# Gating the second batch's adapters on VectorE, ScalarE and GpSimd during the first FFN

## The chip, the cores and the metric

The kernel runs on one NeuronCore of a Trainium2 chip. The metric is device time in microseconds (us), the median of the runs. The engines are TensorE (PE in the profile, with PEld for its weight loads), VectorE (DVE), ScalarE (ACT), GpSimd (POOL) and the queues that issue transfers, above all SyncE's (SP) and ScalarE's.

## What is computed

For each of two batches of 1024 tokens and 2048 features, x is normalised, quantised and multiplied by a quantised context matrix, and added to itself. The result is normalised again and goes through a linear layer with two low-rank adapters, one of its own and one shared. Each batch is split into four groups of 256 tokens, and each group has its own adapter, a gated sum over 16 stored ones of rank 32:

```python
x = x + matmul(fake_quant(layernorm(x)), fake_quant(ctx))        # ctx: (2, 2048, 2048)
z = layernorm(x)                                                 # eight groups of 256 tokens
A_eff = einsum('bn,nri->bri', gate, lora_A)                      # gate: (8, 16), lora_A: (16, 32, 2048)
B_eff = einsum('bn,nor->bor', gate, lora_B)
delta = einsum('bor,btr->bto', B_eff, einsum('bri,bti->btr', A_eff, z))
delta += the same with lora_A_shared and lora_B_shared
x = x + z @ kernel + bias + delta                                # kernel: (2048, 2048), float32
```

`A_eff` and `B_eff` are what the change is about.

## The kernel before

The batches run one after the other, each with an attention stage and an FFN stage. Part of the second batch's attention is already done in the last pass of the first FFN (`meanwhile`).

**Attention.** `quantise` turns loaded 512 KB pieces of the context into bf16 (ACT L314, DVE L317); `xattn_pair` (L350) multiplies one group of 256 tokens with 512 columns of it: ACT fills PSUM with the constant term (L359), PE runs 32 bf16 matmuls (L361), DVE adds the result to `y` (L370) and takes statistics (L372). Towards the end `prep_z` (L422) normalises a group (DVE L428), PE transposes it (L432), ACT copies it out (L433), and it is stored to `zs` in DRAM (L439).

**Adapters.** `gated` (L376) weighs the 16 stored adapters on PE. The stored rows are loaded so that one matmul with a sparse matrix of gates (`gmat`) sums over all 16 for four groups at once; four such matmuls (L383) give 512 columns of `A_eff` or of `B_eff`. DVE copies the sum out (L395). `lora_a_step` (L398) lets PE transpose it (L403) and DVE put it into `acat` (L406); `lora_b_step` (L411) stores it to the DRAM buffer `bd` with eight small transfers on the SP queue (L416). There are four steps of each kind for each batch, between the pairs of the third and fourth block of columns. Their loads stand in the list `todo` among those of the context. `lora_ax` (L442) then multiplies `z` with `acat` on PE.

**FFN.** `ffn` (L635) runs a product of the Strassen kind twice over: seven outer passes (`OUTER`) of seven inner products (`INNER`), 49 products for each batch, each of eight float32 matmuls of 128x128 by 512 on PE (L611, two records each). Operands are sums or differences of blocks. Those of `w` lie in nine buffers `big` and are combined on DVE, with both inputs in SBUF (L551 for the two-term blocks, L560 for the combinations t1 to t4). Those of `z` lie in ten buffers `lit` and are combined on POOL in the same two lines (s1 to s4). `spread` (L620) adds a finished product from PSUM to one or two places of `y` (DVE L629). `Delta.step` (L466) brings in the adapter term after the products 0, 1, 3 and 4 of the first four passes: bias and `bd` are loaded on the ACT queue (L473, L476), ACT writes the bias to PSUM (L478), PE adds four small products (L483), and DVE adds them to `y` (L493).

**The order.** The tile scheduler puts each engine's instructions in a fixed order when the kernel is built; it may bring an instruction forward of its place in the program. `line` (L499) takes this freedom from the DVE instructions that pass through it: each gets an order edge to the one before. POOL's are not bound by it. In a product's step the order is: combinations of the running pass (`OWN`), combinations for the next pass (`AHEAD`), `spread`, `Delta.step`, two-term blocks for the next pass (`BLOCKS`), then the release of buffers and the next loads on SP (`DROP`, `BEGIN`). The block b21 of the next pass comes after the last product's spread, and PE needs it for the second product of that pass.

Of the kernel before, what the change touches and what calls it, by code (L numbers as in the profile page):

```python
# [20 lines left out]
P = 128  # L21
# [45 lines left out]
def tile_quant_xattn_then_lora_ffn(  # L67
# [56 lines left out]
    st1 = const.tile([P, MT, NN, 6], F32, tag="st1", name="st1")  # L124
    st2 = const.tile([P, MT, NN, 6], F32, tag="st2", name="st2")
    r_s = const.tile([P, MT], F32, tag="r_s", name="r_s")

    zs = [
# [11 lines left out]
    def flat(t):  # L140
        return t.rearrange("p k n -> p (k n)")
# [14 lines left out]
    for b in range(B):  # L156
        for n in range(2):
            todo.extend((b, raw_src(b, n, r)) for r in range(KT // 2))
        for n in range(2, 4):
            for r in range(KT // 2):  # L160
                todo.append((b, raw_src(b, n, r)))
                if r in ((3, 7) if n == 2 else (5, 7)):
                    todo.extend((b, ad_src(la, 2 * (n - 2) + r // 6 if n == 3 else r // 4, h)) for h in range(2))
        for n in range(NN):
            todo.extend((b, ad_src(lb, n, h)) for h in range(2))
    loaded = deque()
    ahead = [2]
# [274 lines left out]
    def lora_ax(b, pr, zqs):  # L442
# [12 lines left out]
                )  # L455
        nc.scalar.copy(axT[:, pr, :], px)

    class Delta:


# [37 lines left out]

    def line(ins):  # L499

        if ins.ins.engine == mybir.EngineType.DVE:
            if line.last is not None:
                tc.add_manual_dep(
                    ins.ins,
                    line.last.name,
                    mybir.DependencyInfo(mybir.DependencyClass.NoSync, mybir.DependencyReason.DATA),
                    reason="line",
                )
            line.last = ins.ins

    line.last = None

    NO = len(OUTER)
    last_use = {}
# [120 lines left out]
    def ffn(b, ops, meanwhile):  # L635

        delta = Delta(b)
        for o in range(NO):
            nxt = Operands(b, o + 1) if o + 1 < NO else None
            chains = {}  # L640
            for s in range(len(INNER)):
                product(b, o, s, ops, chains)
                if s in OWN:
                    OWN[s](ops)
                if nxt and s in AHEAD:
                    AHEAD[s](nxt)
                spread(b, o, s, chains)
                if s in (0, 1, 3, 4):
                    delta.step()
                added = line.last  # L650
                if nxt:
                    for name in BLOCKS.get(s, ()):
                        nxt.block(name)
                for name in DROP.get(s, ()):
                    ops.drop(name)
                if nxt:
                    for name in BEGIN.get(s, ()):
                        nxt.load(name)
                with tc.issue_after(added):
                    meanwhile(o, s)  # L660
            ops = nxt
# [31 lines left out]
    for b in range(B):  # L693
# [30 lines left out]
        for g in range(2, GPB):  # L724
            for m in range(g * MG, (g + 1) * MG):
                with tc.issue_after(opened.ins):
                    prep_x(b, m, c1T, wk)
            for n in range(2):
                xattn_pair(b, n, g, c1T, c2[n])
                if g + 1 == GPB:  # L730
                    close_c2(n)
                    open_c2(n + 2)
                    bp.give(colt.pop(n))
                    if n == 0:
                        for r in range(NR):
                            quantise(c2[2], r)
                            if r % 4 == 3:
                                lora_a_step(b, r // 4)
                        column_term(b, 2, c2[2])
        if b == 0:  # L740
            for pr in range(GPB // 2):
# [12 lines left out]
        lora_b_step(b, 0)  # L754
        close_c2(2)
        bp.give(colt.pop(2))
        first = Operands(b, 0)
# [2 lines left out]
        for g in range(GPB):  # L760
# [149 lines left out]
```

## Time and profile before

| | |
|---|---|
| median of 3 runs | 1127.66 us (1126.64 to 1129.02) |
| profiled execution, its own time | 1128.61 us |
| its span | 1126.8 us |
| busy in the span: PE / DVE / ACT / POOL | 1072.4 / 741.5 / 261.1 / 266.6 us |
| first FFN, 300 to 350 us: PE / DVE / ACT / POOL busy | 50.00 / 38.39 / 3.05 / 19.83 us |
| second attention, 650 to 700 us: the same | 49.13 / 26.74 / 19.07 / 0.00 us |
| second attention, 700 to 750 us: the same | 49.39 / 31.26 / 12.99 / 2.22 us |
| granted TensorE clock | 1.00 in all these stretches |

The first attention lasts to about 232 us, the first FFN to about 582 us with the second batch's attention begun from about 542, the second attention to about 782 us, and the second FFN to the end. A row of the profile gives line, engine, operation and tile with shapes, the number of instructions, their busy time and the mean of one, and the idle time before them with what ended it. In a timeline a row is start, length, engine, line and what is written from what; neighbours of the same kind are merged (x3), and a bracket gives the idle time before. A line can be that of a helper: L551 and L560 stand both for DVE and for POOL.

### The profile page before, as it was taken

The numbers are of one execution on the slowest core, as the hardware profiler recorded it, in microseconds if no ns is written. First come the engines' busy times: TensorE is split into PE (matmuls) and PEld (weight loads), VectorE is DVE, ScalarE is ACT, GpSimd is POOL, SyncE is SP. The second block draws the span as 40 slices with busy tenths as digits, with TensorE's granted clock in tenths as the row PEclk, the third lists the DMA queues.
The fourth block names the chain that finished last, engine by engine and source line by source line (L and its number), as shares of the span: only waits on it lengthen the run. The fifth ranks groups of instructions, "written<-read, shape, count | busy, mean of one in ns | idle before, by whom it ended". The sixth has DMA issues, their size and how long they took to land.

```text
span 1126.8 us, 10619 instructions
## 1 busy us (share of the span) xinstructions
PE 1072.4 (95%) x3926; PEld 489.3 (43%) x3926; DVE 741.5 (66%) x969; ACT 261.1 (23%) x342; POOL 266.6 (24%) x106
## 2 busy tenths in 40 slices
PE   1689899999999999999999999999999999999998
PEld 0244334554444444444444433455444444444443
DVE  4685547576696768568777654766668586865861
ACT  5875513320001010001375761232000000000000
POOL 0000000234253422525000000022535343243600
PEclk9999999999999999999999999999999999999999
DMA  8991935885789757489857094588668875749611
GB/s 307 391 244 35 282 124 217 298 322 205 246 285 377 266 181 264 141 301 355 285 184 228 1 277 154 182 301 314 244 215 293 295 255 181 256 145 322 213 38 56
DMA packets 120772, 261.35 MB, mean 232 GB/s; under 512 B 11920, under 2 KB 16144, under 8 KB 119568
## 3 DMA queue, kind: packets, MB, share of 16 engines
q1 hardware_dynamic: 99264, 218.65, 56.6%
q10 hardware_dynamic: 21456, 42.02, 10.5%
q8 instruction: 31, 0.51, 0.2%
q14 instruction: 21, 0.17, 0.0%
HBM read 224.99 MB, written 37.75 MB: 233 GB/s over the span
## 4 chain that ended last, share of the span: by engine, by line
PE 80%; DMA 7%; DVE 6%; ACT 4%; issue 1%; SPq 1%; ACTq 0%; DVEq 0%
PE fu L611 33%; PE fv L611 17%; PE pa L361 13%; PE fw L611 9%; DMA lit<-in_ctx_dram 4%; PE pl L483 3%; PE ptz L432 2%; DVE big L560 1%; PE pg_a L383 1%; DVE st L283 1%; PE pg_b L383 1%; ACT big L298 1%; ACT big L295 1%; DMA bd<-q2b 1%; DMA big<-in_w_dram 1%
## 5 line engine op out<-in xcount | busy, mean ns | idle before, releaser
L611 PE MATMUL fu<-big,lit 128*128 128x512 f32 x896 | 396.3, 594 | 2.4 <-DVE y L629 2.4
L560 POOL TENSOR_TENSOR lit<-lit,lit 128x1024 f32<-128x1024 f32 x56 | 165.2, 2957 | 539.4 <-PE pa L361 209.1
L611 PEld LDWEIGHTS fu<-big,lit 128*128 128x128 f32 x896 | 167.8, 190 | 208.2 <-issue 206.7
L361 PE MATMUL pa<-big,big 128*128 128x512 bf16 x1024 | 238.0, 382 | 11.9 <-ACT pa L359 10.6
L611 PE MATMUL fv<-big,lit 128*128 128x512 f32 x448 | 198.1, 594 | 0.0
L551 POOL TENSOR_TENSOR lit<-lit,lit 128x1024 f32<-128x1024 f32 x40 | 100.9, 2524 | 283.4 <-DMA lit<-zs 255.5
L560 DVE TENSOR_TENSOR big<-big,big 128x2048 f32<-128x2048 f32 x56 | 159.4, 2850 | 5.9 <-PE ptz L432 5.3
L361 PEld LDWEIGHTS <-big 128*128 128x128 bf16 x1024 | 97.0, 98 | 146.5 <-issue 44.3
L629 DVE TENSOR_TENSOR y<-y,fu 128x1024 f32<-128x1024 f32 (+1 forms) x98 | 113.7, 1194 | 67.2 <-PE fu L611 66.8
L611 PEld LDWEIGHTS fv<-big,lit 128*128 128x128 f32 x448 | 84.3, 190 | 105.0 <-issue 105.0
L629 DVE TENSOR_TENSOR y<-y,fv 128x1024 f32<-128x1024 f32 x48 | 56.8, 1218 | 91.1 <-PE fv L611 91.1
L478 ACT COPY pl<-bias 128x1024 f32<-128x1024 f32 x32 | 32.6, 1017 | 344.9 <-DVE y L493 327.1
L314 ACT ACTIVATE q2b<-lit,sc,inv 128x1024 int16<-128x1024 f32 x64 | 76.6, 1230 | 146.4 <-DMA lit<-in_ctx_dram 124.7
L551 DVE TENSOR_TENSOR big<-big,big 128x2048 f32<-128x2048 f32 x40 | 101.7, 2544 | 13.2 <-DMA big<-in_w_dram 13.2
L611 PE MATMUL fw<-big,lit 128*128 128x512 f32 x224 | 100.6, 596 | 0.1
L370 DVE SCALAR_TENSOR_TENSOR y<-pa,k_s,y 128x1024 f32<-128x1024 f32 x32 | 41.0, 1282 | 69.7 <-PE pa L361 69.7
L359 ACT ACTIVATE pa<-bp,r_s 128x512 f32<-128x512 f32 x64 | 42.8, 684 | 105.6 <-PE pa L361 60.5
L629 DVE TENSOR_TENSOR y<-y,fw 128x1024 f32<-128x1024 f32 x24 | 28.4, 1217 | 52.5 <-PE fw L611 52.5
L611 PEld LDWEIGHTS fw<-big,lit 128*128 128x128 f32 x224 | 41.3, 190 | 48.7 <-issue 48.2
L303 PE MATMUL pt<-ident_h,big 128*128 128x128 bf16 x256 | 20.3, 231 | 29.6 <-ACT big L298 29.4
L283 DVE BATCH_NORM_STATS2 st<-y 128x6 f32<-128x512 f32 x64 | 42.1, 680 | 2.9 <-DMA y<-in_x_dram 2.9
L317 DVE TENSOR_SCALAR big<-q2b 128x1024 bf16<-128x1024 int16 x64 | 27.6, 440 | 23.7 <-ACT q2b L314 20.5
(79 smaller groups left out, 609.9 us busy)
## 6 DMA issues: line engine op xcount, KB each, us to landing
big<-in_w_dram SPq DMA_DIRECT2D x96, 1024.0 KB
lit<-zs SPq DMA_DIRECT2D x88, 512.0 KB
lit<-in_ctx_dram SPq DMA_DIRECT2D x64, 512.0 KB
out_dram<-y ACTq DMA_DIRECT2D x30, 512.0 KB
zs<-lit ACTq DMA_DIRECT2D x24, 512.0 KB
y<-in_x_dram SPq DMA_DIRECT2D x8, 1024.0 KB
lit<-in_lora_a_dram SPq DMA_DIRECT2D x32, 256.0 KB
lit<-in_lora_bt_dram SPq DMA_DIRECT2D x32, 256.0 KB
```

What stands on the lines that cost most here:

```text
L283: nc.vector.bn_stats(st1[:, m, n, :], ym[:, ds(n * NB, NB)])
L314: nc.scalar.activation(qi, t, AF.Relu, bias=z2, scale=inv2)
L317: nc.vector.tensor_scalar(c2[r // 4][:, ds(2 * (r % 4), 2), :], qi, QMAX, CENTRE, ALU.min, ALU.subtract)
L359: nc.scalar.activation(pa[:, j, :], colt[n], AF.Identity, bias=r_s[:, m : m + 1])
L361: nc.tensor.matmul(pa[:, j, :], c1T[g][:, k, ds(j * P, P)], c2[k // 8][:, k % 8, :], start=False, stop=(k == KT - 1), skip_group_check=True,)
L370: summed = nc.vector.scalar_tensor_tensor(yp, pa, s12, yp, ALU.mult, ALU.add)
L478: nc.scalar.copy(pl, self.bb.unsqueeze(1).to_broadcast([P, 2, NB]))
L483: nc.tensor.matmul(pl[:, i, ds(h * (NB // 2), NB // 2)], axT[rows, pr, ds(j * P, P)], self.bp[rows, ds(h * (NB // 2), NB // 2)], start=Fal ...
L551: line(eng.tensor_tensor(got[0], got[0], got[1], ALU.add if terms[1][2] > 0 else ALU.subtract))
L560: line(eng.tensor_tensor(out_t, at[p], at[q], op))
L611: nc.tensor.matmul(ps[:, m, :], at[:, k, ds(m * P, P)], bt[:, k, :], start=(opens and k == 0), stop=(ends and k == KQ - 1), skip_group_che ...
L629: line(nc.vector.tensor_tensor(yp, yp, chains[chain][:, js, :], ALU.add if sign > 0 else ALU.subtract))
```

## The change

For the second batch the gated sums are formed without matmuls, during the first batch's FFN. A new class `Gates` takes one step after each product. In products 0 to 15 it loads one stored B adapter each (256 KB, SP queue), and one product later adds it to the accumulators of the four groups, which lie in `acat`: for two groups DVE does a fused multiply and add, for the other two ACT multiplies into a spare buffer and POOL adds. Then the sums go to `bd` with one copy and one transfer a group on ACT. From product 18 the A adapters follow in the same way, and in products 35 to 38 each group's sum is transposed on PE (`turn`), with a copy on ACT before and after. The buffers are a ring of four of 512 columns: the three `q2b` and the statistics buffer, now one tile.

The DVE and POOL instructions of `Gates` pass through `line`, and `line` now keeps an order for POOL too, in both FFNs. `gate_b`, which was overwritten with masked gates, is loaded once more on SP during the first attention. For the second batch `lora_a_step`, `lora_b_step` and their loads are left out; the first batch keeps them.

```diff
+    st = const.tile([P, NB], F32, tag="st", name="st")
+    st1, st2 = (st[:, ds(i * MT * NN * 6, MT * NN * 6)].rearrange("p (m n s) -> p m n s", n=NN, s=6) for i in range(2))
...
-                if r in ((3, 7) if n == 2 else (5, 7)):
+                if b == 0 and r in ((3, 7) if n == 2 else (5, 7)):
...
-        for n in range(NN):
+        for n in range(NN if b == 0 else 0):
...
+    class Gates:
+        OWN = (2, 2, 2, 2, 2, 2, 2)
+        def __init__(self, b):
+            self.b = b
+            self.slot = 0
+            self.held = deque()
+            self.bufs = [q2b.take() for _ in range(len(q2b.spare))]
+            self.ring = Bufs([st] + [flat(t).bitcast(F32) for t in self.bufs])
+        def acc(self, g):
+            return acat[:, :, own_col[g], :]
+        def load(self, src, n):
+            t = self.ring.take()
+            nc.sync.dma_start(out=t, in_=src[ds(n * R, R), :].rearrange("r (c i) -> (r c) i", i=NB))
+            self.held.append(t)
+        def add(self, o, n):
+            t = self.held.popleft()
+            tv = t.rearrange("p (k r) -> p k r", r=R)
+            for g in range(GPB):
+                gw = gate_b[:, self.b * GPB + g, n : n + 1]
+                if g >= self.OWN[o]:
+                    if n == 0:
+                        nc.scalar.mul(self.acc(g), tv, gw)
+                        continue
+                    tmp = self.ring.take()
+                    nc.scalar.mul(tmp, t, gw)
+                    line(
+                        nc.gpsimd.tensor_tensor(
+                            self.acc(g), self.acc(g), tmp.rearrange("p (k r) -> p k r", r=R), ALU.add
+                        )
+                    )
+                    self.ring.give(tmp)
+                elif n == 0:
+                    line(nc.vector.tensor_scalar(self.acc(g), tv, gw, None, ALU.mult))
+                else:
+                    line(nc.vector.scalar_tensor_tensor(self.acc(g), tv, gw, self.acc(g), ALU.mult, ALU.add))
+            self.ring.give(t)
+        def store(self, gs):
...
+        def turn(self, g):
+            t = self.ring.take()
+            nc.scalar.copy(t.rearrange("p (k r) -> p k r", r=R), self.acc(g))
+            pt = ps_m.tile([P, KQ, P], F32, tag="pm", name=f"pgt_{self.b}_{g}")
+            for k in range(KQ):
+                nc.tensor.transpose(pt[:, k, :], t[:, ds(k * P, P)], ident)
...
+        def step(self, o):
+            s = self.slot
+            self.slot += 1
+            if s < NL:
+                self.load(lora_bt, s)
+            if 1 <= s < NL + 1:
+                self.add(o, s - 1)
+            if s == NL + 1:
+                self.store(range(GPB))
+            s -= NL + 2
+            if 0 <= s < NL:
+                self.load(lora_a, s)
+            if 1 <= s < NL + 1:
+                self.add(o, s - 1)
+            if NL + 1 <= s < NL + 1 + GPB:
+                self.turn(s - NL - 1)
...
     def line(ins):
-        if ins.ins.engine == mybir.EngineType.DVE:
...
+        eng = ins.ins.engine
+        if eng in line.last:
...
     def ffn(b, ops, meanwhile):
         delta = Delta(b)
+        gates = Gates(b + 1) if b + 1 < B else None
...
                 if s in (0, 1, 3, 4):
                     delta.step()
-                added = line.last
+                added = line.last[mybir.EngineType.DVE]
+                if gates:
+                    gates.step(o)
                 if nxt:
                     for name in BLOCKS.get(s, ()):
                         nxt.block(name)
...
-                            if r % 4 == 3:
+                            if b == 0 and r % 4 == 3:
                                 lora_a_step(b, r // 4)
...
+            nc.sync.dma_start(
+                out=gate_b.rearrange("p b n -> p (b n)"),
+                in_=gate.rearrange("b n -> (b n)").partition_broadcast(P),
+            )
...
-            if 1 <= g <= 2:
+            if b == 0 and 1 <= g <= 2:
                 lora_a_step(b, g + 1)
...
-        lora_b_step(b, 0)
+        if b == 0:
+            lora_b_step(b, 0)
...
-            if g < 3:
+            if b == 0 and g < 3:
                 lora_b_step(b, g + 1)
```

More of the change, by code (lines that the diff above doesn't have):

```diff
@@ L123, in tile_quant_xattn_then_lora_ffn @@
     gmat = const.tile([P, 2, GPB // 2, RC], F32, tag="gmat", name="gmat")
-    st1 = const.tile([P, MT, NN, 6], F32, tag="st1", name="st1")
-    st2 = const.tile([P, MT, NN, 6], F32, tag="st2", name="st2")
+    st = const.tile([P, NB], F32, tag="st", name="st")
+    st1, st2 = (st[:, ds(i * MT * NN * 6, MT * NN * 6)].rearrange("p (m n s) -> p m n s", n=NN, s=6) for i in range(2))
     r_s = const.tile([P, MT], F32, tag="r_s", name="r_s")
@@ L456, in lora_ax @@
         nc.scalar.copy(axT[:, pr, :], px)
+    class Gates:
[35 more added lines that the diff above has]
+        def store(self, gs):
+            for g in gs:
+                t = self.ring.take()
+                nc.scalar.copy(t.rearrange("p (k r) -> p k r", r=R), self.acc(g))
+                nc.scalar.dma_start(out=bd[self.b][g, g % 2].rearrange("r (c i) -> (r c) i", i=NB), in_=t)
+                self.ring.give(t)
+        def turn(self, g):
+            t = self.ring.take()
+            nc.scalar.copy(t.rearrange("p (k r) -> p k r", r=R), self.acc(g))
+            pt = ps_m.tile([P, KQ, P], F32, tag="pm", name=f"pgt_{self.b}_{g}")
+            for k in range(KQ):
+                nc.tensor.transpose(pt[:, k, :], t[:, ds(k * P, P)], ident)
+            self.ring.give(t)
+            nc.scalar.copy(
+                self.acc(g).rearrange("p (c k) r -> p c k r", c=NN),
+                pt.rearrange("p k (r c) -> p c k r", c=NN),
+            )
[15 more added lines that the diff above has]
+                self.turn(s - NL - 1)
+                if s == NL + GPB:
+                    for t in self.bufs:
+                        q2b.give(t)
@@ L499, in line @@
     def line(ins):
-        if ins.ins.engine == mybir.EngineType.DVE:
[L502 to L511, printed above, removed]
+        eng = ins.ins.engine
+        if eng in line.last:
+            tc.add_manual_dep(
+                ins.ins,
+                line.last[eng].name,
+                mybir.DependencyInfo(mybir.DependencyClass.NoSync, mybir.DependencyReason.DATA),
+                reason="line",
+            )
+        line.last[eng] = ins.ins
+    line.last = {}
     NO = len(OUTER)
@@ L740, in tile_quant_xattn_then_lora_ffn @@
         if b == 0:
+            nc.sync.dma_start(
+                out=gate_b.rearrange("p b n -> p (b n)"),
+                in_=gate.rearrange("b n -> (b n)").partition_broadcast(P),
+            )
             for pr in range(GPB // 2):
```

## The prediction

> **What bounds the kernel now.** I read the page's busy times first, then the chain that ended last, then the timelines of PE, DVE and POOL in the stages that the change touches, and the waits for each.
>
> ```profile
> PE 1072.4 (95%) x3926; PEld 489.3 (43%) x3926; DVE 741.5 (66%) x969; ACT 261.1 (23%) x342; POOL 266.6 (24%) x106
> ```
>
> PE is the bound, but the other shares are means over unlike stages. In the second batch's attention (640 to 782 us) PE idles about 4 us, and the chain runs through the matmuls that are to go. Its lines are start, length, what:
>
> ```profile
> 644.14 0.97 PE pg_a L383 x2
> ...
> 648.67 0.99 PE pg_a L383 x6
> ...
> 651.92 0.44 PE pga L403 x4
> 652.36 0.99 PE pg_a L383 x8
> ```
>
> In the first FFN PE is busy without a gap from 250 to 548 us, so anything late for it there is paid in full. I call the seven passes of its outer loop o0 to o6, the seven products of each s0 to s6, and the end of a product E0 to E6. The tightest pass is o1, whose products end at 286.4, 294.5, 302.6, 309.5, 317.6, 325.7 and 332.5 us. The timelines of DVE, POOL and PE there:
>
> ```profile
> 311.89 1.28 DVE L493 TENSOR_TENSOR y<-pl,y 128x512 f32<-128x512 f32 x2
> 313.08 3.01 DVE L551 TENSOR_TENSOR big<-big,big 128x2048 f32<-128x2048 f32 x1
> 316.13 4.32 DVE L560 TENSOR_TENSOR big<-big,big 128x2048 f32<-128x2048 f32 x1
> 320.37 2.34 DVE L629 TENSOR_TENSOR y<-y,fu 128x1024 f32<-128x1024 f32 x2
> ...
> 328.14 2.29 DVE L551 TENSOR_TENSOR big<-big,big 128x2048 f32<-128x2048 f32 x1
> 330.46 2.29 DVE L560 TENSOR_TENSOR big<-big,big 128x2048 f32<-128x2048 f32 x1
> 332.74 2.35 DVE L629 TENSOR_TENSOR y<-y,fu 128x1024 f32<-128x1024 f32 x2
> 335.01 3.09 DVE L551 TENSOR_TENSOR big<-big,big 128x2048 f32<-128x2048 f32 x1
> ```
>
> ```profile
> 311.59 11.09 POOL L560 TENSOR_TENSOR lit<-lit,lit 128x1024 f32<-128x1024 f32 x3
> 333.59 2.36 POOL L551 TENSOR_TENSOR lit<-lit,lit 128x1024 f32<-128x1024 f32 x1 [10.91 <-DMA lit<-zs]
> ```
>
> ```profile
> 325.67 13.90 PE L611 MATMUL fu<-big,lit 128*128 128x512 f32 x32
> 339.50 1.13 PE L483 MATMUL pl<-bp,axT 64*128 64x256 f32 x8
> 340.56 4.99 PE L611 MATMUL fw<-big,lit 128*128 128x512 f32 x11
> ```
>
> Two things are to be seen. First, DVE operations with both operands in SBUF and POOL operations exclude each other: alone they take 2.28 and 2.36 us, but where three POOL ones meet two DVE ones they take 11.09 and 3.01 + 4.32. They alternate, one whole instruction at a time; L629 and L493, which read PSUM, are not held up. Second, the block that ends at 338.10 (335.01 + 3.09) makes b21 for o2's second product, which starts at 340.56: the margin is 2.5 us. From E5 on DVE never rests there.
>
> **The change, part by part.** *Removed from the second attention:* seven groups of gating matmuls for each adapter, 14 groups of about 0.985 us (one of them off the chain), makes 13.8; four groups of transposes of 0.44 make 1.8. In sum 15.6 us of PE. DVE loses 8 copies of 0.68 and 16 of 0.28 (10 us), which were beside PE. From the SP queue go 32 loads of 256 KB and 32 stores of 32 KB; the ACT queue waited 10.4 us for those stores, and PE 1.1 us behind it, with 0.2 elsewhere. That goes too: 16.9 at most. These matmuls were also filler while DVE and ACT prepared the next pair, so some of it reappears as idle PE. I take 15, with ends 12 and 17.
>
> *Moved to the first FFN:* 32 loads of 256 KB on SP, one a product, in products 0 to 15 and 18 to 33 of the 49. They add 0.26 MB per 7 us, 36 GB/s on 214 to 314, while the DMA engines are 0.61 to 0.85 busy in o1 to o4; no DVE instruction waits for a load there, and each gate load has a whole product in which to land. I cost them at nothing. Their cover is that product; without it DVE would stand in its fixed order, and the blocks behind it. SP could be held by a full ring, since each load reuses a buffer that POOL freed a product earlier; that is bounded by the range. One reload of the gates (453 ns of issue in the row of the first) and four stores on the ACT queue in o2: nothing.
>
> *Added to DVE:* two operations of 128x512 per gated product. The row for 128x512 with a PSUM operand is 0.683 us (L493); the SBUF row 2.28 for 2048 less three times 0.533 (the step between 512 and 1024 in L493 and L629) gives 0.68. I take 0.68; the fused L370 (1282 against 1217 ns at 1024) would make it 0.71. *Added to ACT:* two multiplications of 128x512, about 0.6 us (L433: 588 ns, from PSUM); ACT is under 10% busy there. Behind them on ACT stand the L478 copies that fill PSUM for the delta matmuls on PE; in the walk below they are due 3 to 4 us after they can run, so they cost nothing. *Added to POOL:* two additions, half of 2.36, so 1.2 us each. POOL's order is now fixed as DVE's is, so its blocks stand behind the gate additions. The last addition of a product needs a buffer that DVE's gate additions of the product before have released.
>
> *What this does to o1.* DVE's own work from E0 to the b21 block is seven spreads of 2.35 (16.5), four pairs L493 of 1.28 (5.1), 14 gate operations of 0.68 (9.5) and seven blocks and combinations of 2.28 (16.0): 47.1 us. It must still wait 3.7 us for PE early on (3.1 before E1, 0.6 before E2). Walking both fixed orders through that pass by the alternation seen above, DVE is held by POOL eleven times between E2 and the block: 0.4, 1.0, 0.85, 1.0, 0.75, 0.95, 1.75, 1.0, 0.95, 2.0 and 1.05, together 11.7. So b21 is there 62 us after E0, and PE wants it after 54.1 (340.56 - 286.4). PE stands about 8 us. Without a single new conflict it would still be 0.2 late (four gate operations, 2.7 us, lie between E5 and the block, against the margin of 2.5); with everything colliding, 12.
>
> *The other passes.* o3 has the same DVE work but no two-term blocks on POOL; the same walk gives five waits and b21 at 57 against 53: 4 us (0.3 to 7). o2 has half the spreads and gates in five products: its block ends at 389.3 against 393.7 for PE, and that margin of 4.4 meets 2.3 us of gate operations and some 3.6 of waits: 1.5 (0 to 4). o0 and o4 have no two-term blocks on DVE: 1 (0 to 3) for the first loads, which sit among SP's waits at 234 to 266, and 0.5 (0 to 3). The four late transposes of o5 are the removed 4 x 0.44 again: 1.8 (to 2.4, by the 0.60 of the timeline).
>
> *After a long stand.* At 42.31, after a sparse stretch, 16 matmuls took 5.53 us; the same 16 at 48.62 took 3.61, with the granted clock at 1.00 in both windows:
>
> ```profile
> 42.31 5.53 PE L361 MATMUL pa<-big,big 128*128 128x512 bf16 x16 [1.91 <-ACT pa L359]
> 48.62 3.61 PE L361 MATMUL pa<-big,big 128*128 128x512 bf16 x16 [0.78 <-ACT pa L359]
> ```
>
> I add that difference, 2 us, once for o1 (0 to 5, if the other stands draw it too).
>
> [...]
>
> *The sum.* Losses 8 + 4 + 1.5 + 1 + 0.5 + 1.8 + 2 = 18.8, gain 15: 4 us slower. The profiled execution took 1128.61 (span 1126.8), 0.95 above the median of 1127.66; from the median the forecast is 1132. Low ends: 0.2 + 0.3 + 1.8 of loss against 17, 1113; high ends: 12 + 7 + 4 + 3 + 3 + 2.4 + 5 = 36.4 against 12, 1152.
>
> [...]
>
> **The rivals.** *Faster, 1118.* POOL runs its additions while DVE reads PSUM or waits for PE, so that waits almost vanish. For it: DVE reads PSUM for 21.6 of o1's 53 us, and POOL was 23 of 53 us busy in o1 without costing PE anything. Against it: POOL would reach about 40 of 53, and its last addition is released by DVE's gate operations, which puts it right beside DVE's next block. Losses of about 5.5 (1 + 1 + 0.5 + 1 + 0 + 2) against 15. It decides if o1's waits stay under about 4 us.
>
> *Far slower, 1147.* The gate loads or a full ring hold DVE or SP in place, so operands come late as well. For it: SP already waits 56 us for PE and 46 for DVE's L560 before its w loads, and POOL's blocks free the buffers for the zs loads later than now. Against it: o0 to o4 leave each gate load a product's time. One late operand of 3 us in each of the five passes, on top of the forecast: 15 more.
>
> *The PE relief is hollow, 1139.* If the second attention is really set by context loads (the chain has one of 9.7 us at 656.92), only half the 15 arrives. Against it: PE was busy throughout that load, and the adapter loads that stood in the queue among them are gone.
>
> **How the numbers follow.** A difference under 0.2% (2.3 us) is not to be told from none. The forecast's case (1126 to 1138) has 0.46, the faster 0.28, the far slower 0.14, the hollow relief 0.12. The forecast's own low part gives 0.15 to no change; so faster 0.28, same 0.15, slower 0.57. The range 1116 to 1147 leaves a tenth on either side.
>
> **What would show it.** Right: no gating matmuls between 640 and 770, that stage 13 to 17 us shorter; PE waits on L551 or L560 at o1's and o3's ends, with DVE rows of these lines well over their 2.85 and 2.54 mean, and POOL near 60% busy from 250 to 490. Wrong: a first FFN as dense on PE as now (waits were hidden); PE waits on loads (far slower); an attention stage that shrinks by less than 10 us.

## The result, and the profile after

The changed kernel takes 1157.03 us (median of 4 runs, 1154.59 to 1159.13), against 1127.93 for the kernel before on the same chip: a ratio of 1.0258, 95% interval 1.0234 to 1.0282. The forecast was 1132 in a range of 1116 to 1147: the sign was right, the size was missed by 25 us.

The profiled execution took 1154.59 us (span 1152.8), which is 2.4 under the median, so the readings below account for 26.0 of the 29 us. The busy times of the engines:

```profile
PE 1069.2 (93%) x3832; PEld 493.2 (43%) x3862; DVE 820.3 (71%) x1009; ACT 313.4 (27%) x418; POOL 388.8 (34%) x166
```

PE lost only 3 us of busy time. DVE gained 79 and POOL 122, although the new operations alone are worth 44 and 75 (60 fused ones of 0.73 on DVE and 60 additions of 1.25 on POOL, the shortest of each), and DVE also lost 10 us of copies. Most of the rest is one engine holding the other. PE is no longer dense: its stands (idle stretches) in the first attention's end, in the first FFN and in o6, from its timeline (start, length, engine, line, what, and in the bracket the idle time before and what ended it):

```profile
215.43 1.15 PE L432 MATMUL ptz<-ident,big 128*128 128x128 f32 x8 [3.73 <-ACT lit L433]
...
355.28 9.43 PE L699 MATMUL fw<-big,lit 128*128 128x512 f32 x16 [10.39 <-DVE big L639]
...
412.98 7.10 PE L699 MATMUL fw<-big,lit 128*128 128x512 f32 x16 [1.66 <-DVE big L639]
...
470.98 9.60 PE L699 MATMUL fw<-big,lit 128*128 128x512 f32 x16 [4.98 <-issue]
...
598.26 0.62 PE L303 MATMUL pt<-ident_h,big 128*128 128x128 bf16 x8 [3.31 <-ACT big L298]
```

L699, L639, L648, L717, L571 and L566 are what L611, L551, L560, L629, L483 and L478 were before. The rows at 355.28, 412.98 and 470.98 are the second products of o2, o3 and o4, each waiting for its block b21. At 470.98 the profile names no releaser, but the row of DVE that makes b21 is `468.61 2.28 DVE L639` and ends there. The stands at 355.28 and 470.98 are also paid at the restart: 9.43 and 9.60 us where the 16 records of such a product take 7.13 without a stand. The granted clock shows why, in windows whose columns are the length, the busy times of PE, PEld, DVE, ACT and POOL, then the clock, the share of the DMA engines and GB/s:

```profile
355.00:358.00 3.00, 2.72 (x4) 1.21 (x5) 3.00 (x2) 0.72 (x1) 2.17 (x2) 0.50 1.05 395
...
471.00:474.00 3.00, 3.00 (x4) 1.45 (x5) 3.00 (x1) 0.72 (x1) 2.17 (x2) 0.50 1.04 395
```

Why b21 is late is to be seen in o1 on DVE, one row of its start and then its end, and on POOL beside that end:

```profile
297.52 1.41 DVE L504 SCALAR_TENSOR_TENSOR acat<-q2b,gate_b,acat 128x512 f32<-128x512 f32 x2
...
327.15 2.34 DVE L717 TENSOR_TENSOR y<-y,fu 128x1024 f32<-128x1024 f32 x2
329.41 1.27 DVE L581 TENSOR_TENSOR y<-pl,y 128x512 f32<-128x512 f32 x2
330.61 3.50 DVE L504 SCALAR_TENSOR_TENSOR acat<-q2b,gate_b,acat 128x512 f32<-128x512 f32 x2
334.03 2.34 DVE L717 TENSOR_TENSOR y<-y,fv 128x1024 f32<-128x1024 f32 x2
336.29 4.45 DVE L504 SCALAR_TENSOR_TENSOR acat<-q2b,gate_b,acat 128x512 f32<-128x512 f32 x2
340.66 2.28 DVE L639 TENSOR_TENSOR big<-big,big 128x2048 f32<-128x2048 f32 x1
342.98 3.23 DVE L648 TENSOR_TENSOR big<-big,big 128x2048 f32<-128x2048 f32 x1
346.13 2.34 DVE L717 TENSOR_TENSOR y<-y,fu 128x1024 f32<-128x1024 f32 x2
348.40 4.53 DVE L504 SCALAR_TENSOR_TENSOR acat<-st,gate_b,acat 128x512 f32<-128x512 f32 x2
352.85 2.28 DVE L639 TENSOR_TENSOR big<-big,big 128x2048 f32<-128x2048 f32 x1
```

```profile
329.53 2.36 POOL L648 TENSOR_TENSOR lit<-lit,lit 128x1024 f32<-128x1024 f32 x1
331.84 1.72 POOL L496 TENSOR_TENSOR acat<-acat,q2b 128x512 f32<-128x512 f32 x1
334.94 1.27 POOL L496 TENSOR_TENSOR acat<-acat,q2b 128x512 f32<-128x512 f32 x1 [1.39 <-ACT q2b L494]
336.16 2.37 POOL L648 TENSOR_TENSOR lit<-lit,lit 128x1024 f32<-128x1024 f32 x1
338.46 1.73 POOL L496 TENSOR_TENSOR acat<-acat,q2b 128x512 f32<-128x512 f32 x1
341.64 2.43 POOL L496 TENSOR_TENSOR acat<-acat,q2b 128x512 f32<-128x512 f32 x1 [1.45 <-ACT q2b L494]
344.02 4.40 POOL L639 TENSOR_TENSOR lit<-lit,lit 128x1024 f32<-128x1024 f32 x1
348.39 2.33 POOL L648 TENSOR_TENSOR lit<-lit,lit 128x1024 f32<-128x1024 f32 x1
350.69 1.70 POOL L496 TENSOR_TENSOR acat<-acat,q2b 128x512 f32<-128x512 f32 x1
```

A pair of gate operations on DVE (L504) takes 1.41 us where POOL rests (the row at 297.52), and 3.50, 4.45 and 4.53 here, beside POOL's blocks, combinations and additions. The spreads (L717), which read PSUM, keep their 2.34. DVE has hardly a gap in the whole pass (64.21 us busy of the 64.55 from 290.58 on). The last row makes b21, and PE's 355.28 follows it.

In the second attention no gating matmul is left. The whole of that stretch, from the last record of the first column sums of the context (`pcp`) to the first product `fv` of the second FFN, before and then after (columns as in the windows above):

```profile
598.54:788.02 189.48, 184.38 (x987) 87.63 (x987) 123.72 (x242) 75.00 (x113) 13.87 (x6) 1.00 0.62 202
```

```profile
633.42:814.06 180.64, 171.85 (x894) 86.59 (x907) 116.47 (x218) 75.03 (x113) 12.17 (x5) 0.99 0.45 157
```

The stretch is 8.8 us shorter. PE's busy time fell by 12.5 and its idle time rose from 5.1 to 8.8: DVE and ACT prepare the next group much as before (ACT is busy 75.03 us of the stretch, 75.00 before), and PE now waits for them (`761.59 ... [2.84 <-DVE big L428]`). Behind that wait the granted clock was 0.64 from 761.5 to 766, which takes up part of the busy time that was saved.

The balance by stretches: +3.2 to the first `fu` behind the last `px` of the first attention (240.96 to 244.17), +31.7 from there to the end of the first FFN (357.58 to 389.25), -8.8 in the second attention, nothing in the second FFN: +26.1 of the span's 26.0.

### The profile page after: what moved, and what is told of

It is laid out like the page before. It is cut to its first block, busy times and chain, and to the rows that moved or that the text cites. A ratio compares the mean times of both kernels' runs of the same rounds, so it can differ in the third digit from the quotient of the medians.

```text
span 1152.8 us, 10674 instructions
## 1 busy us (share of the span) xinstructions
PE 1069.2 (93%) x3832; PEld 493.2 (43%) x3862; DVE 820.3 (71%) x1009; ACT 313.4 (27%) x418; POOL 388.8 (34%) x166
## 5 line engine op out<-in xcount | busy, mean ns | idle before, releaser
L699 PE MATMUL fu<-big,lit 128*128 128x512 f32 x896 | 399.4, 598 | 1.2 <-DVE y L717 1.2
L648 POOL TENSOR_TENSOR lit<-lit,lit 128x1024 f32<-128x1024 f32 x56 | 154.2, 2757 | 627.6 <-DMA zs<-lit 207.7
L699 PEld LDWEIGHTS fu<-big,lit 128*128 128x128 f32 x896 | 168.5, 191 | 206.3 <-issue 204.4
L361 PE MATMUL pa<-big,big 128*128 128x512 bf16 x994 | 231.9, 381 | 11.0 <-ACT pa L359 7.6
L699 PE MATMUL fv<-big,lit 128*128 128x512 f32 x448 | 198.1, 594 | 0.0
L648 DVE TENSOR_TENSOR big<-big,big 128x2048 f32<-128x2048 f32 x56 | 160.0, 2859 | 5.5 <-PE ptz L432 5.0
L717 DVE TENSOR_TENSOR y<-y,fu 128x1024 f32<-128x1024 f32 (+1 forms) x98 | 113.5, 1191 | 46.3 <-PE fu L699 45.7
L639 POOL TENSOR_TENSOR lit<-lit,lit 128x1024 f32<-128x1024 f32 x40 | 126.1, 3162 | 23.3 <-DMA lit<-zs 23.2
L699 PEld LDWEIGHTS fv<-big,lit 128*128 128x128 f32 x448 | 84.2, 190 | 104.5 <-issue 104.5
L699 PE MATMUL fw<-big,lit 128*128 128x512 f32 x224 | 105.2, 620 | 17.5 <-DVE big L639 12.1
L639 DVE TENSOR_TENSOR big<-big,big 128x2048 f32<-128x2048 f32 x40 | 98.2, 2454 | 13.7 <-DMA big<-in_w_dram 10.0
L717 DVE TENSOR_TENSOR y<-y,fv 128x1024 f32<-128x1024 f32 x48 | 56.7, 1216 | 64.7 <-PE fv L699 64.7
L496 POOL TENSOR_TENSOR acat<-acat,q2b 128x512 f32<-128x512 f32 x43 | 78.1, 1818 | 57.8 <-ACT q2b L494 50.2
L566 ACT COPY pl<-bias 128x1024 f32<-128x1024 f32 x32 | 32.5, 1017 | 215.3 <-DVE y L581 199.8
L699 PEld LDWEIGHTS fw<-big,lit 128*128 128x128 f32 x224 | 43.1, 199 | 70.1 <-issue 69.1
L504 DVE SCALAR_TENSOR_TENSOR acat<-q2b,gate_b,acat 128x512 f32<-128x512 f32 x46 | 68.4, 1525 | 0.0
L717 DVE TENSOR_TENSOR y<-y,fw 128x1024 f32<-128x1024 f32 x24 | 28.4, 1215 | 39.7 <-PE fw L699 39.6
```

The costliest lines, as they stand in the source:

```text
L361: nc.tensor.matmul(pa[:, j, :], c1T[g][:, k, ds(j * P, P)], c2[k // 8][:, k % 8, :], start=False, stop=(k == KT - 1), skip_group_check=True,)
L496: nc.gpsimd.tensor_tensor(self.acc(g), self.acc(g), tmp.rearrange("p (k r) -> p k r", r=R), ALU.add)
L504: line(nc.vector.scalar_tensor_tensor(self.acc(g), tv, gw, self.acc(g), ALU.mult, ALU.add))
L566: nc.scalar.copy(pl, self.bb.unsqueeze(1).to_broadcast([P, 2, NB]))
L639: line(eng.tensor_tensor(got[0], got[0], got[1], ALU.add if terms[1][2] > 0 else ALU.subtract))
L648: line(eng.tensor_tensor(out_t, at[p], at[q], op))
```

## The experiments

The theory at first: DVE's gate operations and POOL's additions are late together, because they hold each other. The rivals: the loads on SP, VectorE's own added work, and the queues of ScalarE and POOL. The edits are against the changed kernel unless another is named. "Before" was 1128.06 to 1128.14 us in all sets of runs.

**e1_relief: only the relief.** Nearly nothing is gated in the first FFN.

```diff
-            if s < NL:
+            if s < 1:
                 self.load(lora_bt, s)
-            if 1 <= s < NL + 1:
+            if s == 1:
                 self.add(o, s - 1)
```

and the same for `lora_a`.

> Left out: of the sixteen adapters of the second batch only the first is loaded and gated, so the sums are incomplete; stores, transposes and everything else stay. This is the change without its work in the first FFN. Theory (DVE's and POOL's additions cross each other and make operands late): the first FFN is as dense on PE as in the kernel before except for the four transposes, about +2 us; the second attention gives back the 8.8 us of the changed kernel, not more; the first attention loses nothing, since the ACT multiplication that stood there is gone. In sum 1121 to 1125 us. Rival (the loss has nothing to do with the additions, but with the order and buffers of the new kernel): still over 1140.

Measured: 1123.42 us (1120.36 to 1124.45), ratio 0.9952 [0.9934, 0.9970]. Without its gating work the whole change is worth 4.7 us, not 15. In the profile the second attention is 183.48 us long against 189.48, with PE busy 173.23; the first FFN is 3.3 us longer than before, though hardly anything is gated in it. Of that the four late transposes take 1.7 (0.43 each, from start to start), and the first transposes of o6 wait 2.37 us instead of 0.82; e5 finds out why they do.

**e2_loads: all loads, nothing gated but the first adapter.**

```diff
-            for g in range(GPB):
+            for g in range(GPB if n == 0 else 0):
                 gw = gate_b[:, self.b * GPB + g, n : n + 1]
```

> Left out: all sixteen adapters are loaded, but only the first is gated. Theory: within 2 us of the run with one load, because no operand waits for a transfer. Rival (the 32 loads hold up the SP queue or the operands' transfers): 10 us or more above it, with PE waiting for L639 blocks whose own wait is for a load.

Measured: 1130.22 (1126.62 to 1132.20), ratio 1.0017 [1.0004, 1.0030]; 6.8 us over e1. The FFN is dense; the cost lies ahead of it. The SP queue in the first attention's end:

```profile
206.66 7.84 SPq L480 DMA_DIRECT2D q2b<-in_lora_bt_dram  x3
214.55 0.43 SPq L629 DMA_DIRECT2D big<-in_w_dram  x1
215.08 0.78 SPq L480 DMA_DIRECT2D q2b<-in_lora_bt_dram  x1
215.96 0.43 SPq L480 DMA_DIRECT2D st<-in_lora_bt_dram  x1
216.44 6.90 SPq L480 DMA_DIRECT2D q2b<-in_lora_bt_dram  x3
224.69 0.38 SPq L629 DMA_DIRECT2D big<-in_w_dram  x1
```

With buffers free at once, the scheduler brought four gate loads (the first stands at 204.37, ahead of these rows) forward of the weight load at 214.55 and five more forward of that at 224.69, on the queue that serves both. DVE waits 7.30 us for weights (`222.37 2.29 DVE L639 ... [7.30 <-DMA big<-in_w_dram]`), and PE 5.27 us for that block at 224.72. In the changed kernel the ring is held longer, and two and one gate loads stand there.

**e3_dve_part and e4_pool_part: each engine's share alone.** In e3 VectorE gates its two groups as in the change, and ScalarE and GpSimd only the first adapter; in e4 it is the other way about.

```diff
-            for g in range(GPB):
+            for g in range(GPB if n == 0 else self.OWN[o]):               # e3
+            for g in range(0 if n == 0 else self.OWN[o], GPB):            # e4
```

> Left out: for the two groups of ACT and POOL only the first adapter is gated; DVE does its two operations in every gated product as in the changed kernel. Theory: DVE has 9.5 us more work in the tightest pass, which nearly fills its margin, but meets only the old POOL operations; 0 to 5 us above the run with loads alone, L504 near 0.75 us each. Rival (VectorE's own extra work is what is late): 15 us or more above it.

> Left out: for the two groups of DVE only the first adapter is gated; ACT and POOL do theirs in every gated product. Theory: 3 us return in the first attention, where an early ACT multiplication waits for its load; in the FFN POOL's additions delay DVE's blocks a little; in sum 3 to 7 us above the run with loads alone. The parts above loads alone, DVE's and POOL's, add up to under 12 us, against some 30 for both together. Rival (POOL's additions alone, or the ACT queue behind them, make the loss): 20 us or more above loads alone.

Measured: e3 1131.38 (1126.38 to 1134.36), ratio 1.0025 [1.0012, 1.0039], 1.2 over e2; its stands in o1 are 1.86 and 1.43 us. e4 1172.32 (1170.39 to 1173.54), ratio 1.0390 [1.0372, 1.0407]: half the gating costs more than the whole of it. As a theory of "both together" mine fell. The waits of PE in e4 (total, times, longest), and the ACT queue before one of them:

```profile
PE pl L571 <- ACT pl L566: 30.0, 6, 11.1
```

```profile
262.64 1.33 ACT L494 ACTIVATE q2b<-st,gate_b 128x512 f32<-128x512 f32 x2 [4.04 <-POOL acat L496]
271.73 0.72 ACT L494 ACTIVATE q2b<-q2b,gate_b 128x512 f32<-128x512 f32 x1 [7.75 <-POOL acat L496]
272.36 1.00 ACT L566 COPY pl<-bias 128x1024 f32<-128x1024 f32 x1
```

The multiplication at 271.73 needs a spare buffer and waits 7.75 us for the POOL addition that frees it. The copy that fills the delta tile stands behind it on the same queue, and PE waits 6.16 us for that copy (at 273.41). The scheduler put eight multiplications between the second copy of the FFN and this third one; in the changed kernel, where some of them must also wait for VectorE to release their buffers, it put four there.

**e8_copy_first: e4 with that copy out of the way.** `Delta.step` is cut in two: loads and copy go into `begin`, called at the end of the step before, and both kinds of ACT instruction keep the written order.

```diff
+            line(nc.scalar.copy(pl, self.bb.unsqueeze(1).to_broadcast([P, 2, NB])))
+            self.ready = pr, n, j, cols, pl
...
                 bias_b.give(self.bb)
+            self.begin()
...
-                    nc.scalar.mul(tmp, t, gw)
+                    line(nc.scalar.mul(tmp, t, gw))
```

> As e4_pool_part (VectorE's two groups gated for n = 0 alone), but each ScalarE copy of the bias into the delta tile is issued as soon as the additions of the tile before are out, ahead of the gate multiplications of that product. If the 30 us of TensorE waits on that copy are those of the in-order ScalarE queue behind multiplications that wait for GpSimd, they go: 1138 to 1148. If GpSimd's additions hold the blocks of VectorE instead, the waits only change their name: 1165 or more.

Measured: 1144.04 (1142.53 to 1147.74), ratio 1.0143 [1.0119, 1.0168]: 28 us came back, nearly all of the 30. So most of e4's excess is the ScalarE queue. What remains is 14 us over e2, with a new first line in PE's waits (L708 and L648 are here the products and the blocks):

```profile
PE fw L708 <- POOL lit L648: 11.4, 2, 8.1
```

Now POOL's own blocks are late behind its additions.

**e14_after_copy_first: the same step in the changed kernel.** The edit is that of e8, with all four groups gated.

> The changed kernel with each ScalarE copy into the delta tile issued ahead of the gate multiplications, as in e8_copy_first. If the ScalarE queue costs the changed kernel only the 3.3 us of waits that the profile puts to it: 1151 to 1155. If those waits also set off the stands of o1 and o3: 1140 or less. If they were slack that the stands at the end of the pass swallow: 1156 to 1159.

Measured: 1157.75 (1156.29 to 1160.25), ratio 1.0267 [1.0246, 1.0289], no change. PE's waits:

```profile
PE fw L708 <- POOL lit L648: 14.6, 2, 11.5
PE fw L708 <- issue: 9.7, 1, 9.7
```

The waits on the delta tile fall from 3.3 to 1.3 us, and the early multiplication of the first attention is gone too (the first `fu` behind it at 240.05 instead of 244.17). Yet the stand behind o1 is now 11.54 us instead of 10.39, that behind o3 9.68 instead of 4.98, and one of 3.06 behind o0 is new. In the changed kernel the ACT waits were slack: the passes are set by DVE and POOL, and what PE doesn't wait for in the middle it waits for at the end.

**e6_all_dve: VectorE gates all four groups.**

```diff
-        OWN = (2, 2, 2, 2, 2, 2, 2)
+        OWN = (4, 4, 4, 4, 4, 4, 4)
```

> VectorE gates all four groups itself; ScalarE and GpSimd take no part. By own work: o1 then holds 28 gate operations of 0.7 us instead of 14, so VectorE's work from E0 to the b21 block is 47.1 + 9.5 = 56.6 us, with 3.7 of early waiting 60.3 against the 54.1 at which TensorE wants it, before any meeting with GpSimd; o3 likewise some 5 us late; the ScalarE waits of the delta tile and the early ScalarE multiplication of the first attention go. Sum: 1144 to 1156. By GpSimd's side alone (the DVE part cost 1.2 us by itself, GpSimd's 42): 1132 to 1137, with o1 and o3 dense.

Measured: 1174.13 (1170.60 to 1176.59), ratio 1.0400 [1.0369, 1.0431]. Too much work on VectorE is as bad as too much meeting; it came out above my 1144 to 1156, which left out that POOL's ordinary blocks hold the gate operations too. From 286 to 362 us, 31 gate operations take 33.8 us where 21.9 is their time alone. The lateness shows in PE's waits for the spreads (2.41 at 312.55) and then for the delta tile (`328.26 ... [6.88 <-ACT pl L566]`), which ACT fills only once DVE has read the one before (`327.19 1.02 ACT L566 ... [22.89 <-DVE y L581]`).

**e10_not_o1_o3, e15_o1_o3_dve and e16_o1_o3_pool: only the two tight passes.** In o1 and o3 the additions are left out altogether (e10), those on ScalarE and GpSimd are (e15), or those on VectorE are (e16); the other passes stay as changed.

```diff
-            for g in range(GPB):
+            for g in range(0 if o in (1, 3) else GPB):                    # e10
+            for g in range(self.OWN[o] if o in (1, 3) else GPB):          # e15
+            for g in range(self.OWN[o] if o in (1, 3) else 0, GPB):       # e16
```

> The changed kernel with the gate additions of o1 and o3 left out (lora_bt 6 to 12 and lora_a 2 to 8 are loaded but not added, on any engine). If the loss is VectorE's lateness for b21 in these two passes (stalls 10.4 and 5.0, restarts 2.3 and 2.5, and 1.8 of waits on the delta tile there): 1133 to 1139. If it lies in the ring, the loads or the queues, the additions of o0, o2 and o4 keep most of it: 1148 or more.

> The changed kernel with the ScalarE and GpSimd part of the additions left out in o1 and o3 (groups 2 and 3 of lora_bt 6 to 12 and lora_a 2 to 8 are not added); VectorE's part stays there. If GpSimd's additions holding VectorE's blocks make the stands: 1138 to 1142. If VectorE's own 14 operations per pass make them: 1150 or more.

> The changed kernel with VectorE's part of the additions left out in o1 and o3 (groups 0 and 1 there); ScalarE and GpSimd keep theirs. If the meetings of GpSimd's additions with the blocks are enough by themselves, or its buffers hold the ScalarE queue as in e4_pool_part: 1148 or more. If it takes both parts together to be late: 1136 to 1142.

Measured: e10 1137.27 (1135.39 to 1139.63), ratio 1.0080 [1.0057, 1.0102]; e15 1140.36 (1140.11 to 1141.26), ratio 1.0112 [1.0097, 1.0128]; e16 1160.58 (1159.29 to 1163.46), ratio 1.0299 [1.0277, 1.0321]. So 20 of the 29 us are made in o1 and o3. 17 of them go with the part of ScalarE and GpSimd alone, and VectorE's 14 operations a pass cost only 3. In e15 the end of o1 is:

```profile
347.82 8.80 PE L699 MATMUL fw<-big,lit 128*128 128x512 f32 x16 [2.37 <-DVE big L639]
```

2.37 where the changed kernel stood 10.39. In e16, without VectorE's part to hold the buffers, PE's waits on the ACT copy return (22.0 us in all, the longest 11.1), as in e4.

**e5_pool_line: the written order of POOL alone.** The kernel before, with `line` as in the change and no `Gates`.

> The kernel before with one part of the change alone: GpSimd's instructions keep the written order as VectorE's do; nothing is gated elsewhere. If the fixed order costs by itself (in o5 a combination waits 23 us for TensorE in front of the blocks, the first context load of o6 starts some 4 us later and TensorE waits 2.4 us for the first transposes): 1130 to 1133, with that wait at the end of the first FFN. If the order costs only together with gate additions: 1127 to 1129.

Measured: 1130.47 (1127.69 to 1132.20), ratio 1.0019 [1.0008, 1.0030]: 2.4 us for an order edge. POOL in o5, in e5 and in the kernel before (L560 the combination, L551 the blocks):

```profile
499.17 2.36 POOL L560 TENSOR_TENSOR lit<-lit,lit 128x1024 f32<-128x1024 f32 x1 [22.99 <-PE fw L611]
501.50 6.72 POOL L551 TENSOR_TENSOR lit<-lit,lit 128x1024 f32<-128x1024 f32 x2
```

```profile
487.83 2.36 POOL L551 TENSOR_TENSOR lit<-lit,lit 128x1024 f32<-128x1024 f32 x1 [10.47 <-DMA lit<-zs]
499.49 2.35 POOL L551 TENSOR_TENSOR lit<-lit,lit 128x1024 f32<-128x1024 f32 x1 [9.30 <-DMA lit<-zs]
501.80 2.36 POOL L560 TENSOR_TENSOR lit<-lit,lit 128x1024 f32<-128x1024 f32 x1
```

Without the edge POOL made a block at 487.83, while a combination waited for PE. With it the combination stands in front. `lit` buffers come free later, SP issues the first context load of o6 at 524.03 instead of 518.91, and the first transposes wait 3.20 us for ACT and then run at 1.03 instead of 0.62:

```profile
565.75 1.03 PE L303 MATMUL pt<-ident_h,big 128*128 128x128 bf16 x8 [3.20 <-ACT big L298]
```

This is the stand at 598.26 of the changed kernel, and with the four late transposes what e1's first FFN lost.

**e11_pool_free: the changed kernel without the written order of POOL.**

```diff
-        if eng in line.last:
+        if eng in line.last and eng == mybir.EngineType.DVE:
```

> The changed kernel with GpSimd's instructions left to the scheduler's order (only VectorE's order is written). If the fixed order costs what it shows in o6 and no more: 1151 to 1155, with the lateness of o1 and o3 kept. If GpSimd's additions held blocks mainly because of the fixed order: 1145 or less. If the scheduler's order lets additions and blocks meet worse: 1158 or more.

Measured: 1160.44 (1158.97 to 1165.57), ratio 1.0275 [1.0260, 1.0291]. The stand at o6 shrinks to 0.82, but the scheduler now sets POOL's blocks and combinations ahead of the additions (508.10 to 516.53 on POOL's timeline). The last A addition ends at 529.63, and the first late transpose waits 9.14 us behind it. The stand behind o1 is shorter without the edge (7.61 for 10.39), that behind o3 longer (5.50 for 4.98). The intervals of the two kernels overlap, and this profiled execution, at 1165.57, is the slowest of the five; so that the edge gains anything while gating goes on is not shown, only that dropping it everywhere saves nothing.

**e9_a_only, e12_a_only_pool_free and e13_a_only_o0_o4: a version from these findings.** Only A is gated in the first FFN, in the products that showed hardly a stall; B stays on PE, where its matmuls fill time anyway. Gate loads get an order edge behind the operand loads of their product. e9 keeps POOL's written order, e12 drops it, e13 keeps it in o0 to o4 alone.

```diff
+        SLOTS = {0: range(1, 7), 2: range(4), 4: range(7)}
...
+            if s not in self.SLOTS.get(o, ()):
+                return
+            n = self.slot
+            self.slot += 1
+            if n < NL:
+                self.load(lora_a, n)
+            if 1 <= n < NL + 1:
+                self.add(o, n - 1)
...
-        if b == 0:
-            lora_b_step(b, 0)
+        lora_b_step(b, 0)
...
+        if eng in line.last and (eng == mybir.EngineType.DVE or line.pool):   # e13
...
+            line.pool = gates is not None and o < NO - 2                      # e13
```

> Only lora_a of the second batch is gated in the first FFN, two groups on VectorE and two on ScalarE and GpSimd as in the change, in o0 (products 1 to 6), o2 (0 to 3) and o4 (0 to 6), where the changed kernel showed hardly a stall; lora_bt of that batch is gated on TensorE in the second attention as before; gate loads are issued behind the operand loads of their product. If the change's 8.8 us of gain in the second attention lie in the pg_a part, and its cost in o1 and o3: 1119 to 1124. If the gain needs both adapters gone: 1126 to 1130. If the gate work costs in every pass: 1130 or more.

> As e9_a_only, with GpSimd's instructions left to the scheduler's order. If the fixed order is what gives back some 3 us of e9_a_only's gain at the end of the first FFN: 1123 to 1126. If the scheduler sets additions ahead of blocks that TensorE needs: 1129 or more.

> As e9_a_only, with GpSimd's written order kept only in o0 to o4 of the first FFN, where the gate additions are, and the scheduler's order elsewhere. By the same theory 1123 to 1126, with the first transposes of o6 waiting under 1.5 us; if the lateness at o6 comes from the four late transposes and the buffers given back in o5: 1127 to 1129, as e9_a_only.

Measured: e9 1128.11 (1126.30 to 1129.28), ratio 0.9996 [0.9987, 1.0005]; e12 1124.51 (1123.97 to 1125.99), ratio 0.9965 [0.9953, 0.9977]; e13 1123.01 (1121.02 to 1125.07), ratio 0.9951 [0.9938, 0.9964]. e9 missed its expectation for two reasons: its second attention gains 6.8 us and not 8.8, and its FFN loses the o6 stand of 3.51 us (e5's), the slow restart behind it (the transposes at 1.03 again) and the four late transposes. With the order edge confined to the passes that need it, that stand is 0.82, as in the kernel before:

```profile
567.68 0.62 PE L303 MATMUL pt<-ident_h,big 128*128 128x128 bf16 x8 [0.82 <-ACT big L298]
```

e13 is faster than both kernels, 5 us under the one before, and about equals e1 with B's matmuls still on PE. Its second attention is 180.40 us long, that of e12 180.81: as short as the 180.64 of the changed kernel, which has none of B's matmuls there.

## Why the prediction was wrong

The terms of the sum, in us; what was measured is from the rows of the two profiles.

| step | predicted | measured |
|---|---|---|
| gain of the second attention | 15 (12 to 17) | 8.8 |
| o1, stand for b21 | 8 (0.2 to 12) | 10.4, and 1.0 on the delta tile |
| o3, the same | 4 (0.3 to 7) | 5.0, and 0.9 |
| o2, the same | 1.5 (0 to 4) | 1.7, and 0.5 |
| o0 / o4 | 1 / 0.5 | 0 / 0.5 |
| four late transposes | 1.8 (to 2.4) | 2.5 |
| slow restart | 2, once (to 5) | 2.3 and 2.5 |
| first attention | 0 | 3.2 |
| o6, first transposes | 0 | 2.5, and 1.7 in the restart |
| loss | 18.8 | 34.7 |

*Right: the bound and the mechanism.* b21 at the end of o1, then o3, then o2 was named, in that order, and the stands lie within their ends. DVE and POOL do hold each other for whole instructions while PSUM readers pass (L504 1.41 alone, 4.53 beside POOL; L717 2.34 or 2.35 for each pair of o1). VectorE's own work without new meetings was put 0.2 late; with its operations alone e3 stood 1.43 there. The walk of o1 found 11.7 us of holding, and the profile has 16.2 up to b21: 13.3 on gate operations, 3.0 on blocks. Of the 16.2, 2.9 lie before E2, where the walk had no holds but 3.7 us of waiting for PE, which is gone; POOL was busy for 51 of these 64.5 us, where the text expected 40 of 53. The holds are longer than the stand of 10.4, and e15 shows that without the work of ScalarE and GpSimd in o1 it shrinks to 2.37.

*Wrong: the gain of 15.* The step "some of it reappears as idle PE" was sized at 1.9 (16.9 less 15). e1 shows 4.7 of 15.6 for the whole kernel, and 6.0 in the second attention; the changed kernel gained 8.8 there. The rival of the hollow relief, at half, was nearer, but for another reason than its context loads: waits for DVE (L428) and a slow restart behind the longest filled part of the space. e12 and e13 show the same from the other side: with B's matmuls left on PE the stretch is as short.

*Wrong: what was costed at nothing.* "Loads: nothing" named a cover, a whole product for each load, but the scheduler may issue a load as soon as its buffer is free. In e2 they went ahead of the weights and cost 6.8 us; in the changed kernel a gate multiplication also came forward on ACT and waited 4.05 us for its load, with the copies of the transposes (L433) behind it: the stand of 3.73 at 215.43. "POOL's order is now fixed" was noted, with gate additions in mind, but what else stands in that order was not followed through o5 and o6; e5 prices it at 2.4. Last, "L478 copies cost nothing" is wrong by the waits (3.3 us in all) and held in the time, since e14 takes 2.0 of them away and is no faster; but that is luck: the same queue costs 28 us in e4 against e8.

*The clock.* The forecast took one slow restart, for o1, and left any other to its high end. That its 2 us fit the measured 2.3 and 2.5 is luck: they came from a row whose granted clock was 1.00, and the restarts here ran at 0.50. Behind the stands of 10.39 and 4.98 the granted clock was 0.50 from 355 to 359.5 and from 471 to 476 us, and back at 1.00 and 0.99 in the windows from 360 and 476; behind that of 1.66 it was 1.00 for the whole product (7.10 at 412.98). So both long stands paid where the sum had one of them pay. How long a stand must be for that, these three do not show; the last section has those of the other runs.

Of the rivals, the faster one would have needed holds under 4 us in o1, and the hollow relief had one half of the sum right and left the loss untouched. The one that was nearest in time, far slower at 1147, named a full ring as its cause; e4 shows that such a ring can hold ScalarE, e14 that in the changed kernel it decides nothing. What the range lacked was that gain and loss could both err to the same side: 6 us less gain and 16 more loss, half of that outside the passes that were walked.

Two things stay open. The median is 2.4 us over the profiled execution, and which stretch makes that difference is not shown; single stretches do differ: e5, which has nothing else of the change than POOL's order, ends the first attention at 239.26 us where the profile of before has 240.96, and e1 at 237.18. So the 3.2 of the first attention is known only within some us, though the stand of 3.73 is plain in its rows. And in the first attention PE waits 2.16 us for `pa` behind a late context load in the profile of before, and in e6 and e10 similarly, but not in that of after; no experiment was made on it.

## What to carry to other kernels

Work taken off the bounding engine is worth its time only where nothing else is due in that stretch: ask which engine prepares the next piece, and how much of the removed work only filled its wait. Work moved to "idle" engines must be walked through the queues that they share: here VectorE and GpSimd excluded each other (4.53 us for a pair of gate operations that took 1.41 where GpSimd rested), ScalarE kept a short copy behind a multiplication that waited 7.75 us for a buffer (e4), and SP took early loads ahead of urgent ones, so that DVE waited 7.30 us for weights (e2). An order edge is a change by itself; put it only where it is needed, and measure it alone.

## What the runs showed that was not expected

Half of the moved work can cost more than the whole: the part of ScalarE and GpSimd alone took 1172 us, both parts 1157. With VectorE's operations holding the buffers, fewer multiplications were put ahead of the copy that TensorE needs. An order edge between instructions that do nothing new cost 2.4 us.

The length of a stand alone did not tell whether the restart was slow. Stands on the product matmuls between 2.16 and 2.63 us went either way: those of 2.16 and 2.41 (e6) and 2.37 us (e15) were followed by 8.83, 8.83 and 8.80 us for a product that takes 7.13, those of 2.17 (e14) and 2.63 us (e6) by 7.11 and 7.13. Behind that of 2.16 the granted clock was 0.57 (508 to 512 us), behind those of 2.17 and 2.63 it was 1.00. All longer ones in the changed kernel, e2, e6, e11 and e14 were followed by a slow product, from 2.93 (e6) and 3.06 us (e14) on, with 8.80 and 8.62. It also came late: after 3.44 us in e4 the delta matmuls still ran at their 1.13 with a granted clock of 1.00, and the product behind them began at 0.55 (426.6 to 430 us) and took 8.83:

```profile
425.62 1.13 PE L571 MATMUL pl<-bp,axT 64*128 64x256 f32 x8 [3.44 <-ACT pl L566]
426.69 8.83 PE L699 MATMUL fu<-big,lit 128*128 128x512 f32 x16
```
